# A two-layer sequence model on one core: the second stream yields after each whole-array product, scans weigh less in the mix, and the experts' gate rows come by repeating transfers

## The chip, the cores and the metric

The kernel runs on one core of a Trainium2 chip. Five engines work side by side: TensorE for matrix products (PE, its weight loads are shown as PEld), VectorE (DVE), ScalarE (ACT), GpSimd (POOL) and SyncE (SP), which here only issues transfers. The metric is the device time of one execution in microseconds (us); lower is better. All data are 32-bit floats, except where a product is made in the one-pass format that the code calls F32R.

## The reference

The input is one sequence of 2048 tokens of width 128. Two layers follow, each an attention-like part and a feed-forward part on a residual:

- Layer 0, first part: layernorm, a Mamba-2 style state space block (8 heads of 32, state 16) with a causal convolution of four taps, a gate, a skip path, and an output projection.
- Layer 0, second part: layernorm, causal attention with 16 heads of 8, then layernorm and a mixture of 8 experts of width 512. Every expert is computed for every token. A token's two largest gate logits are put through a softmax and the other six gates are zero, so an expert's output is multiplied by a gate that differs from token to token: `y = sum over e of gate[token, e] * (gelu(x W1[e] + b1[e]) W2[e] + b2[e])`.
- Layer 1, first part: layernorm and a Mamba-1 style scan: 256 channels with 16 states each, `h[t] = exp(-(n+1) delta[t]) * h[t-1] + delta[t] B_n[t] u[t]`, summed over the 16 states, times a gate, and projected.
- Layer 1, second part: layernorm and a feed-forward part of width 512: silu-gated first products, two 512x512 layers with gelu, and a projection to 128.

## The kernel before

**Chunks and stages.** The 2048 tokens are cut into four chunks of 512, numbered 0 to 3. On the chip an activation is held as 128 channels by 512 tokens, so one "whole-array product" is a 128x128 weight against 128x512 activations into one PSUM bank. The stages are Python generators: `ssd(c)` for layer 0's state space block, `attentions()` for all of the attention, `experts(c)`, `scan(c)` and `feed(c)`. At each `yield w` a generator hands over control and says with `w` roughly how much work it has recorded since its last yield. What is recorded then goes through a scheduler that may still move instructions of independent stages past each other, and each engine runs its own list in order.

**Attention is the thread through the middle.** It walks over (chunk, group of four heads). `shift` computes scores once (L302) and takes row maxima on DVE (L312). `weighted` computes scores again, transposed (L352), adds the shift by a product (L358), masks the diagonal (L360), takes `exp` on ACT (L362), and multiplies the result with the values (L339). Each `weighted` step handles two heads by 512 queries by 128 keys. There are 320 such steps over the whole kernel, and only one PSUM buffer, `ps_e`, for their scores, so a step's scores can't be written before the `exp` of the step before has been read out.

**The second stream.** While attention runs, the other stages are mixed in by `with_attention(stages, rate)`: for each `w` that a stage yields, the attention is advanced by `w * rate`. First `ssd(1..3)` are mixed in, then `second_layers()`: `experts(0)`, then `scan(0)` beside `experts(1)`, then `scan(1)` beside `feed(0)`, then `experts(2)`, then `feed(1)`. Two stages are put side by side by `abreast`, which always advances the one that has done the smaller share of its total. When attention is over, the tail runs: `scan(2)` beside `experts(3)`, `scan(3)` beside `feed(2)`, then `feed(3)` alone. Chunk 3's experts need the whole attention; `scan(3)` needs `experts(3)` and the last states of `scan(2)`; `feed(3)` needs `scan(3)`.

**One expert** (in `experts`) loads its weights (256 KB each, L780 and L781), makes four first products (L789) with a `gelu` each (L790), yields 3.7, makes four second products into one bank (L794), multiplies by the gates (L796), adds to the sum on POOL (L798), and yields 3.5. The gates lie with tokens on partitions; the multiplication needs one expert's gates as a row repeated over all 128 partitions. Before, that is made on TensorE: the gates are transposed twice over (L762), split into a high and a low part (L772, L773) so that the one-pass format loses nothing, kept as 16 rows (`rows_in`, L774), and for each expert a one-pass product with a column of ones and zeros (`spread_row`, L719) fills a PSUM bank that DVE copies out (`gb`, L785). `scan` gets its rows `bb` in another way: it writes them to DRAM once (`scratch_b`, L840) and reads each back with a transfer whose source row is repeated for all partitions (L861).

**Tables.** `gelu` and `silu` on the one side and `exp` on the other need different ACT tables, and each change is an ACT_TABLE_LOAD. `in_turn` keeps the recorded order between `gelu` and `exp`, so that they don't alternate at will; how often the recorded order alternates is up to the yields.

**Queues.** SP issues all weight loads, `scratch_b` and `bb` in order; a transfer that waits for its buffer holds up those behind it. POOL issues the transfers that accumulate the scan's sums in SBUF (L876).

Of the kernel before, what the change touches and what calls it, by code (L numbers as in the profile page):

```python
# [12 lines left out]
F32 = mybir.dt.float32  # L13
# [6 lines left out]
P = 128  # L20
# [52 lines left out]
def two_layers(ctx: ExitStack, tc: tile.TileContext, a: dict, out: bass.AP):  # L73
# [375 lines left out]
    attending_all = attentions()  # L449

    SSD, MOE, SCAN, FEED = 43.0, 62.0, 46.0, 40.0
    RATE = (4 * 11.0 + sum(48.0 * (c + 1) for c in range(NC))) / (2.5 * SSD + 2 * (MOE + SCAN + FEED) + 0.6 * MOE)


    with ExitStack() as first:
# [233 lines left out]

    w_eg = load(wp, "w_eg", [P, NE])  # L690
    w_in1 = load(wp, "w_in1", [P, 4 * P])
    w_bd = load(wp, "w_bd", [P, 2, 3 * DS], "(k p) o -> p k o", p=P)
    w_u = load(wp, "w_u", [P, 2, DI], "(k p) o -> p k o", p=P)
    w_dt1 = load(wp, "w_dt1", [3 * DS, DI])
    w_out1 = load(wp, "w_out1", [P, 2, D], "(k p) o -> p k o", p=P)

    halo1 = wp.tile([P, 2, 3], F32, name="halo1")
# [1 line left out]
    hlast = wp.tile([P, 2, DS], F32, name="hlast")  # L699
    nc.gpsimd.memset(hlast, 0.0)  # L700


    zeros = side.line("zeros")
    nc.gpsimd.memset(zeros, 0.0)
    two_rows, minus_low, rows_in = {}, {}, {}
    scratch_b = [tc.dram_tile([DS, C], F32, name=f"scratch_b{i}") for i in range(2)]
    for n in (NE,):
        two_rows[n] = wp.tile([P, n], F32R, name=f"two_rows{n}")
        nc.vector.tensor_tensor(two_rows[n], ident[:, 0:n], ident[:, n : 2 * n], ALU.add)
        minus_low[n] = wp.tile([2 * n, 2 * n], F32R, name=f"minus_low{n}")  # L710
        nc.vector.tensor_scalar(minus_low[n], ident[0 : 2 * n, 0 : 2 * n], 0.0, None, ALU.mult)
        nc.vector.tensor_scalar(minus_low[n][:, n:], ident[0 : 2 * n, n : 2 * n], -1.0, None, ALU.mult)
        rows_in[n] = [wp.tile([P, C], F32R, name=f"rows_in{n}_{i}") for i in range(1)]
        for t in rows_in[n]:
            nc.vector.tensor_copy(t, zeros)

    def spread_row(pg, n, rows_of, i):

        nc.tensor.matmul(pg, two_rows[n][:, i : i + 1].to_broadcast([P, P]), rows_of, start=True, stop=True)  # L719


    def experts(c, z):
        yield from after_stage(("attention", c))
        x = xc[c]
        nx = z.blocks("xn")
        layernorm(nx, xa[c])
        pt = transposed(nx, z.bank)
        nT = z.line("nT")
        nc.vector.tensor_scalar(nT, pt, col("ln2_w"), col("ln2_b"), ALU.mult, ALU.add)
        yield 1.0  # L730

# [24 lines left out]
        nc.vector.reciprocal(top, top)  # L756
        ge2 = sp.tile([P, NB, 2, NE], F32, tag="ge2", name="ge2")
        for i in range(2):
            nc.vector.tensor_tensor(ge2[:, :, i], ge, top.unsqueeze(2).to_broadcast([P, NB, NE]), ALU.mult)
        pgt = z.bank([2 * NE, C])  # L760
        for b in range(NB):
            nc.tensor.matmul(  # L762
                pgt[:, b * P : (b + 1) * P],
                ge2[:, b].rearrange("p i e -> p (i e)"),
                ident,
                start=b == 0,
                stop=True,
                skip_group_check=b > 0,
            )
        gT = rows_in[NE][0]  # L770
        ghi = z.line("ghi", (2 * NE, C), F32R)
        nc.vector.tensor_copy(ghi, pgt)  # L772
        nc.tensor.matmul(pgt, minus_low[NE], ghi, start=False, stop=True, skip_group_check=True)  # L773
        nc.vector.tensor_copy(gT[0 : 2 * NE], pgt)  # L774
        yield 1.5

        acc = z.line("acc")
        for e in range(NE):
            we = z.wide()
            nc.sync.dma_start(we[:, 0], a["fc1"][e])  # L780
            nc.sync.dma_start(we[:, 1].rearrange("p (k d) -> p k d", k=NF), a["fc2"][e].rearrange("(k p) d -> p k d", p=P))  # L781
            pg = z.bank([P, C])
            spread_row(pg, NE, gT, e)
            gb = z.line("gb")
            nc.vector.tensor_copy(gb, pg)  # L785
            hs = [z.four("h") for _ in range(2)]
            for f in range(NF):
                ph = z.bank([P, C])
                nc.tensor.matmul(ph, we[:, 0, f * P : (f + 1) * P], nT, start=True, stop=True)  # L789
                in_turn("gelu", nc.scalar.activation(hs[f // 2][:, f % 2, :], ph, AF.Gelu, bias=col("fc1_b", e * NF + f)))  # L790
            yield 3.7
            py = z.sum([P, C])
            for f in range(NF):
                nc.tensor.matmul(py, we[:, 1, f * P : (f + 1) * P], hs[f // 2][:, f % 2, :], start=f == 0, stop=f == NF - 1)  # L794
            dst = acc if e == 0 else z.line("ye")
            nc.vector.scalar_tensor_tensor(dst, py, col("fc2_b", e), gb, ALU.add, ALU.mult)  # L796
            if e:
                nc.gpsimd.tensor_tensor(acc, acc, dst, ALU.add)  # L798
            yield 3.5
        pt = z.bank([P, NB, D])  # L800
        for b in range(NB):
            nc.tensor.transpose(pt[:, b, :], acc[:, b * P : (b + 1) * P], ident)
        nc.vector.tensor_tensor(x, x, pt, ALU.add)
        yield 1.0


    def scan(c, z):
# [22 lines left out]
            nc.scalar.activation(xs[:, j, :], xs[:, j, :], AF.Silu, bias=col("conv_b", j))  # L830
        yield 4.5

        pb = z.bank([3 * DS, C])
        for k in range(2):
            nc.tensor.matmul(pb, w_bd[:, k, :], xs[:, k, :], start=k == 0, stop=k == 1)
        bd = z.line("bd", (3 * DS, C))
        nc.vector.tensor_scalar(bd, pb, col("bd_b", 0, 3 * DS), None, ALU.add)

        rows_b = scratch_b[c % 2]
        nc.sync.dma_start(rows_b, bd[0:DS])  # L840
# [55 lines left out]
    def feed(c, z):  # L896
# [12 lines left out]
        for f in range(NF):  # L909
# [4 lines left out]
            s = z.line("s")  # L914
            in_turn("gelu", nc.scalar.activation(s, p1, AF.Silu, scale=col("w1_s", f)))
            nc.vector.scalar_tensor_tensor(h[f // 2][:, f % 2, :], p2, col("w2_s", f), s, ALU.mult, ALU.mult)
        yield 7.0
        for name, scale in (("h1", "h1_s"), ("h2", "h2_s")):
            w = []
            for i in range(2):  # L920
# [3 lines left out]
            for f in range(NF):  # L924
                ph = z.bank([P, C])
                for k in range(NF):
                    nc.tensor.matmul(  # L927
                        ph, w[k // 2][:, k % 2, f * P : (f + 1) * P], h[k // 2][:, k % 2, :], start=k == 0, stop=k == NF - 1
                    )
                in_turn("gelu", nc.scalar.activation(g[f // 2][:, f % 2, :], ph, AF.Gelu, scale=col(scale, f)))  # L930
                if f % 2:
                    yield 7.0
            h = g
        po = z.sum([P, NB, D])
        for b in range(NB):
# [9 lines left out]

    def abreast(*threads):

        live = [[g, n, 0.0] for g, n in threads]
        while live:
            for t in sorted(live, key=lambda t: t[2] / t[1]):  # L950
                try:
                    w = next(t[0])
                except StopIteration:
                    live.remove(t)
                    break
                if w is not None:
                    t[2] += w
                    yield w
                    break
            else:  # L960
                yield None

    def second_layers():
        yield from experts(0, side)
        yield from abreast((scan(0, scans), SCAN), (experts(1, side), MOE))
        yield from abreast((scan(1, scans), SCAN), (feed(0, side), FEED))
        yield from experts(2, side)
        yield from feed(1, side)

# [12 lines left out]
def _layout(L0_attn_u, **w):  # L982
# [12 lines left out]
    W_in = w["L0_attn_W_in"]  # L995
    Wqkv, bqkv = w["L0_ffn_Wqkv"], w["L0_ffn_bqkv"]
    x_proj, x_b = w["L1_attn_x_proj_w"], w["L1_attn_x_proj_b"]
    order = np.r_[DS : 2 * DS, DS : 2 * DS, 0:DS]
    bd_b = np.zeros((P, 1), f)
    bd_b[: 3 * DS, 0] = x_b[order]  # L1000
    w_dt1 = np.zeros((3 * DS, DI), f)
    w_dt1[2 * DS :] = w["L1_attn_dt_proj_w"]
    col = {
        "ln_gamma": cols(w["L0_attn_ln_gamma"]),
        "ln_beta": cols(w["L0_attn_ln_beta"]),
# [73 lines left out]
```

## Time and profile before

| | before |
|---|---|
| median of 3 runs | 1753.18 us (1751.92 to 1757.4) |
| the profiled execution's own time | 1741.55 us |
| its span from first to last instruction | 1739.8 us |
| granted TensorE clock, mean | 0.837 |
| busy share of the span: PE, PEld, DVE, ACT, POOL | 84%, 36%, 56%, 42%, 16% |
| attention's last add to the residual (L396) starts at | 1420.0 us |
| transfers | 83.24 MB, mean 48 GB/s |

The profiled execution is 0.67% quicker than the median, so a sum made against the profile is carried to the median by that factor. The shares are means over stages with different limits; the end of the attention at 1420 us cuts the execution in two parts that have to be read apart. A busy PE is not a PE at full speed[...].

### The profile page before, as it was taken

The page shows a single profiled execution, that of the slowest core. Times are in us where ns is not written, and L with a number is a line of the kernel's source. Part 1 is how long each engine was busy: PE and PEld are TensorE (multiplying, and loading weights), DVE is VectorE, ACT ScalarE, POOL GpSimd, SP SyncE. Part 2 cuts the span into 40 slices and gives each one's busy share as a digit, 9 for nine tenths or more (in the row PEclk, how much of TensorE's full clock was granted, in tenths as well). Part 3 has the DMA queues.
Part 4 walks back from the last instruction along what each step waited for, and adds up shares of the span by engine and source line. Part 5 has one row for each costly group of instructions (what it writes and reads, how often), then busy time and mean ns, then how long its engine had stood idle before and what let it go on. Part 6 is the DMA issues. An engine that isn't in the chain of part 4 may idle for free. (4 is left out here: it accounts for less than half of the span.)

```text
span 1739.8 us, 16427 instructions
## 1 busy us (share of the span) xinstructions
PE 1466.9 (84%) x6306; PEld 633.5 (36%) x6306; DVE 975.0 (56%) x1556; ACT 726.2 (42%) x847; POOL 284.0 (16%) x316
## 2 busy tenths in 40 slices
PE   6898999998999888888978887789999888658528
PEld 3554545444333333232333322433333233223214
DVE  4566646557344565667466686674442036774950
ACT  2222322322445444555354454355563536534522
POOL 3322210211000100112111021110000001440220
PEclk9898997887899978889677898669996899868859
DMA  2000000001000000324220045320011022860841
GB/s 85 1 1 1 1 1 1 1 1 55 24 25 25 25 13 21 83 49 103 55 49 14 30 99 107 68 42 25 24 37 31 24 67 78 178 125 31 188 96 30
DMA packets 62494, 83.24 MB, mean 48 GB/s; under 512 B 4576, under 2 KB 28816, under 8 KB 62416
## 3 DMA queue, kind: packets, MB, share of 16 engines
q0 software_dynamic: 16320, 31.46, 10.4%
q1 hardware_dynamic: 45664, 49.68, 9.7%
q8 instruction: 49, 0.80, 0.2%
q10 hardware_dynamic: 432, 1.06, 0.2%
q14 instruction: 29, 0.24, 0.0%
HBM read 49.55 MB, written 1.18 MB: 29 GB/s over the span
## 5 line engine op out<-in xcount | busy, mean ns | idle before, releaser
L362 ACT ACTIVATE probs<-ps_e 128x1024 f32<-128x1024 f32 (+3 forms) x320 | 286.6, 896 | 505.8 <-PE ps_e L358 304.0
L312 DVE TENSOR_REDUCE top<-ps_m 128x2 f32<-128x1024 f32 (+3 forms) x320 | 339.7, 1062 | 280.8 <-PE ps_m L302 164.1
L302 PE MATMUL ps_m<-kR,qR 32*128 32x512 f32 (+3 forms) x640 | 190.1, 523 | 68.0 <-DVE top L312 55.2
L352 PE MATMUL ps_e<-qR,kR 32*128 32x512 f32 (+3 forms) x640 | 175.5, 519 | 27.5 <-ACT probs L362 26.8
L339 PE MATMUL ps_o<-probs,vv 128*9 128x512 f32 (+3 forms) x1152 | 169.7, 599 | 1.0 <-ACT probs L362 0.9
L302 PEld LDWEIGHTS ps_m<-kR,qR 32*128 32x128 f32 x640 | 78.6, 208 | 242.9 <-DVE top L312 132.1
L867 DVE TENSOR_TENSOR_SCAN db<-da,hlast,db 128x512 f32<-128x512 f32 x128 | 163.0, 1310 | 6.5 <-ACT da L863 4.7
L358 PE MATMUL ps_e<-sh,onesR 32*128 32x512 f32 (+3 forms) x640 | 148.9, 431 | 0.0
L352 PEld LDWEIGHTS ps_e<-qR,kR 32*128 32x128 f32 x640 | 69.7, 204 | 182.0 <-ACT probs L362 106.3
L789 PE MATMUL ps_a<-nT,wide 128*128 128x512 f32 x192 | 113.8, 699 | 6.0 <-ACT h L790 3.7
L794 PE MATMUL ps_c<-h,wide 128*128 128x512 f32 x192 | 103.5, 643 | 0.0
L798 POOL TENSOR_TENSOR acc<-acc,ye 128x512 f32<-128x512 f32 x28 | 43.6, 1558 | 331.5 <-DVE ye L796 331.5
L871 POOL COPY hlast<-db 128x2 f32<-128x2 f32 x48 | 29.4, 612 | 378.9 <-DVE db L867 378.9
L863 ACT ACTIVATE da<-dl 128x1024 f32<-128x1024 f32 x64 | 66.4, 1054 | 51.5 <-DMA db<-db 28.3
L865 DVE TENSOR_TENSOR db<-du,bb 128x1024 f32<-128x1024 f32 x64 | 77.9, 1227 | 16.3 <-issue 11.0
L790 ACT ACTIVATE h<-ps_a,cols 128x512 f32<-128x512 f32 x96 | 63.8, 686 | 52.2 <-PE ps_a L789 51.9
L358 PEld LDWEIGHTS ps_e<-sh,onesR 32*128 32x128 f32 x640 | 77.2, 219 | 3.2 <-issue 1.8
L927 PE MATMUL ps_a<-g,wide 128*128 128x512 f32 x96 | 54.0, 690 | 19.5 <-ACT g L930 19.5
L789 PEld LDWEIGHTS ps_a<-nT,wide 128*128 128x128 f32 x192 | 37.1, 215 | 46.3 <-issue 19.5
L362 ACT ACT_TABLE_LOAD x41 | 52.6, 1283 | 1.3 <-PE ps_e L358 0.6
L927 PE MATMUL ps_a<-h,wide 128*128 128x512 f32 x96 | 51.1, 665 | 0.8 <-ACT g L930 0.8
L375 DVE COPY os<-ps_o 128x512 f32<-128x512 f32 x16 | 10.9, 684 | 70.8 <-PE ps_o L339 70.7
(375 smaller groups left out, 2129.3 us busy)
## 6 DMA issues: line engine op xcount, KB each, us to landing
wide<-in_fc SPq DMA_DIRECT2D x64, 256.0 KB, 3.2
bb<-scratch_b SPq DMA_DIRECT2D x64, 256.0 KB, 3.5
db<-db POOLq DMA_DIRECT2D x32, 512.0 KB, 5.7
u<-db POOLq DMA_DIRECT2D x28, 512.0 KB, 6.0
wide<-in_h SPq DMA_DIRECT2D x16, 512.0 KB, 3.7
wide<-in_w SPq DMA_DIRECT2D x8, 256.0 KB, 3.1
x<-in_x SPq DMA_DIRECT2D x4, 256.0 KB, 5.1
w<-in_w SPq DMA_DIRECT2D x4, 256.0 KB, 4.0
```

Of the source, the lines that this page charges most:

```text
L302: nc.tensor.matmul(pss[:, j, 0:n], qR[hr, w - P : w], kR[hr, g, kc * C : kc * C + n], start=True, stop=not diag,)
L312: nc.vector.tensor_reduce(top[:, i : i + 2, kc], pss[:, :, 0:n], AX.X, ALU.max)
L339: pv = nc.tensor.matmul(o, v, prs[i // 2][:, i % 2, q0:], start=kb == 0, stop=kb == nk - 1)
L352: nc.tensor.matmul(pss[:, j, q0:], kR[hr, g, kb * P : (kb + 1) * P], qR[hr, q0:], start=True, stop=False)
L358: nc.tensor.matmul(pss[:, j, q0:], onesR[hr], sh[hr, q0:], start=False, stop=not diag)
L362: last = nc.scalar.activation(pr[:, :, q0:], pss[:, :, q0:], AF.Exp, scale=float(1.0 / np.sqrt(np.float32(HD))))
L789: nc.tensor.matmul(ph, we[:, 0, f * P : (f + 1) * P], nT, start=True, stop=True)
L794: nc.tensor.matmul(py, we[:, 1, f * P : (f + 1) * P], hs[f // 2][:, f % 2, :], start=f == 0, stop=f == NF - 1)
L863: in_turn("exp", nc.scalar.activation(da, dl, AF.Exp, scale=-float(n + 1)))
L865: nc.vector.tensor_tensor(db, du, bb.unsqueeze(1).to_broadcast(two), ALU.mult)
L867: nc.vector.tensor_tensor_scan(db[:, j, :], da[:, j, :], db[:, j, :], hlast[:, j, n : n + 1], ALU.mult, ALU.add)
L927: nc.tensor.matmul(ph, w[k // 2][:, k % 2, f * P : (f + 1) * P], h[k // 2][:, k % 2, :], start=k == 0, stop=k == NF - 1)
```

## The change

It has three parts. First, `experts` and `feed` yield after each whole-array product in a group that accumulates (0.9 each, 0.8 after the last), where they yielded 3.5 or 7.0 after a group; the totals stay the same. Second, `abreast` takes a share for each thread, and what it passes on to the mix with the attention is `w` times the share: 0.3 for scans, 1.0 for the others. The rate is worked out anew from these: it was 524 / 440.7 = 1.19 and becomes 524 / 401.1 = 1.31. The tail's `together` has no shares. Third, the gates are transposed once (8 rows), written to DRAM (`scratch_g`, 16 KB), and each expert reads its row with a transfer that repeats it over the 128 partitions, issued by SP after the expert's two weight loads. The products and copies of `spread_row` go, and so do the high and low parts, and the doubled rows that `w_bd` and `w_dt1` still had (48 rows become 32).

```diff
-    RATE = (...) / (2.5 * SSD + 2 * (MOE + SCAN + FEED) + 0.6 * MOE)
+    RATE = (...) / (2.5 * SSD + 3 * MOE + 0.6 * SCAN + 2.0 * FEED)
...
-    def spread_row(pg, n, rows_of, i):
-        nc.tensor.matmul(pg, two_rows[n][:, i : i + 1].to_broadcast([P, P]), rows_of, start=True, stop=True)
+    scratch_g = [tc.dram_tile([NE, C], F32, name=f"scratch_g{i}") for i in range(2)]
...  experts: the gates
-        ge2 = sp.tile([P, NB, 2, NE], F32, tag="ge2", name="ge2")
-        for i in range(2):
-            nc.vector.tensor_tensor(ge2[:, :, i], ge, top.unsqueeze(2).to_broadcast([P, NB, NE]), ALU.mult)
-        pgt = z.bank([2 * NE, C])
-        for b in range(NB):
-            nc.tensor.matmul(pgt[:, b * P : (b + 1) * P], ge2[:, b]..., ident, ...)
-        gT = rows_in[NE][0]
-        ghi = z.line("ghi", (2 * NE, C), F32R)
-        nc.vector.tensor_copy(ghi, pgt)
-        nc.tensor.matmul(pgt, minus_low[NE], ghi, start=False, stop=True, skip_group_check=True)
-        nc.vector.tensor_copy(gT[0 : 2 * NE], pgt)
+        nc.vector.tensor_tensor(ge, ge, top.unsqueeze(2).to_broadcast([P, NB, NE]), ALU.mult)
+        pgt = z.bank([NE, C])
+        for b in range(NB):
+            nc.tensor.transpose(pgt[:, b * P : (b + 1) * P], ge[:, b], ident)
+        gT = z.line("gT", (NE, C))
+        nc.vector.tensor_copy(gT, pgt)
+        gates = scratch_g[c % 2]
+        nc.sync.dma_start(gates, gT)
...  experts: one expert
-            pg = z.bank([P, C])
-            spread_row(pg, NE, gT, e)
             gb = z.line("gb")
-            nc.vector.tensor_copy(gb, pg)
+            nc.sync.dma_start(gb, gates[e].partition_broadcast(P))
...
                 nc.tensor.matmul(py, we[:, 1, f * P : (f + 1) * P], ...)
+                if f < NF - 1:
+                    yield 0.9
...
-            yield 3.5
+            yield 0.8
...  feed: the first products
-        yield 7.0
+            if f % 2:
+                yield 3.5
...  feed: h1 and h2
                     nc.tensor.matmul(ph, w[k // 2][:, k % 2, f * P : (f + 1) * P], ...)
+                    if k < NF - 1:
+                        yield 0.9
                 in_turn("gelu", nc.scalar.activation(g[f // 2][:, f % 2, :], ph, AF.Gelu, scale=col(scale, f)))
-                if f % 2:
-                    yield 7.0
+                yield 0.8
...  abreast
-                    t[2] += w
-                    yield w
+                    t[3] += w
+                    yield w * t[2]
...
-        yield from abreast((scan(0, scans), SCAN), (experts(1, side), MOE))
-        yield from abreast((scan(1, scans), SCAN), (feed(0, side), FEED))
+        yield from abreast((scan(0, scans), SCAN, 0.3), (experts(1, side), MOE, 1.0))
+        yield from abreast((scan(1, scans), SCAN, 0.3), (feed(0, side), FEED, 1.0))
```

More of the change, by code (lines that the diff above doesn't have):

```diff
@@ L451, in two_layers @@
     SSD, MOE, SCAN, FEED = 43.0, 62.0, 46.0, 40.0
-    RATE = (4 * 11.0 + sum(48.0 * (c + 1) for c in range(NC))) / (2.5 * SSD + 2 * (MOE + SCAN + FEED) + 0.6 * MOE)
+    RATE = (4 * 11.0 + sum(48.0 * (c + 1) for c in range(NC))) / (2.5 * SSD + 3 * MOE + 0.6 * SCAN + 2.0 * FEED)
     with ExitStack() as first:
@@ L691, in two_layers @@
     w_in1 = load(wp, "w_in1", [P, 4 * P])
-    w_bd = load(wp, "w_bd", [P, 2, 3 * DS], "(k p) o -> p k o", p=P)
+    w_bd = load(wp, "w_bd", [P, 2, 2 * DS], "(k p) o -> p k o", p=P)
     w_u = load(wp, "w_u", [P, 2, DI], "(k p) o -> p k o", p=P)
-    w_dt1 = load(wp, "w_dt1", [3 * DS, DI])
+    w_dt1 = load(wp, "w_dt1", [2 * DS, DI])
     w_out1 = load(wp, "w_out1", [P, 2, D], "(k p) o -> p k o", p=P)
@@ L700, in two_layers @@
     nc.gpsimd.memset(hlast, 0.0)
-    zeros = side.line("zeros")
-    nc.gpsimd.memset(zeros, 0.0)
-    two_rows, minus_low, rows_in = {}, {}, {}
+    scratch_g = [tc.dram_tile([NE, C], F32, name=f"scratch_g{i}") for i in range(2)]
     scratch_b = [tc.dram_tile([DS, C], F32, name=f"scratch_b{i}") for i in range(2)]
[L707 to L715, printed above, removed]
-    def spread_row(pg, n, rows_of, i):
-        nc.tensor.matmul(pg, two_rows[n][:, i : i + 1].to_broadcast([P, P]), rows_of, start=True, stop=True)
     def experts(c, z):
@@ L756, in experts @@
         nc.vector.reciprocal(top, top)
-        ge2 = sp.tile([P, NB, 2, NE], F32, tag="ge2", name="ge2")
-        for i in range(2):
-            nc.vector.tensor_tensor(ge2[:, :, i], ge, top.unsqueeze(2).to_broadcast([P, NB, NE]), ALU.mult)
-        pgt = z.bank([2 * NE, C])
+        nc.vector.tensor_tensor(ge, ge, top.unsqueeze(2).to_broadcast([P, NB, NE]), ALU.mult)
+        pgt = z.bank([NE, C])
         for b in range(NB):
[L762 to L769, printed above, removed]
-        gT = rows_in[NE][0]
-        ghi = z.line("ghi", (2 * NE, C), F32R)
-        nc.vector.tensor_copy(ghi, pgt)
-        nc.tensor.matmul(pgt, minus_low[NE], ghi, start=False, stop=True, skip_group_check=True)
-        nc.vector.tensor_copy(gT[0 : 2 * NE], pgt)
+            nc.tensor.transpose(pgt[:, b * P : (b + 1) * P], ge[:, b], ident)
[3 more added lines that the diff above has]
+        nc.sync.dma_start(gates, gT)
         yield 1.5
@@ L831, in scan @@
         yield 4.5
-        pb = z.bank([3 * DS, C])
+        pb = z.bank([2 * DS, C])
         for k in range(2):
             nc.tensor.matmul(pb, w_bd[:, k, :], xs[:, k, :], start=k == 0, stop=k == 1)
-        bd = z.line("bd", (3 * DS, C))
-        nc.vector.tensor_scalar(bd, pb, col("bd_b", 0, 3 * DS), None, ALU.add)
+        bd = z.line("bd", (2 * DS, C))
+        nc.vector.tensor_scalar(bd, pb, col("bd_b", 0, 2 * DS), None, ALU.add)
         rows_b = scratch_b[c % 2]
@@ L946, in abreast @@
     def abreast(*threads):
-        live = [[g, n, 0.0] for g, n in threads]
+        live = [[g, n, share, 0.0] for g, n, share in threads]
         while live:
-            for t in sorted(live, key=lambda t: t[2] / t[1]):
+            for t in sorted(live, key=lambda t: t[3] / t[1]):
                 try:
@@ L997, in _layout @@
     x_proj, x_b = w["L1_attn_x_proj_w"], w["L1_attn_x_proj_b"]
-    order = np.r_[DS : 2 * DS, DS : 2 * DS, 0:DS]
+    order = np.r_[DS : 2 * DS, 0:DS]
     bd_b = np.zeros((P, 1), f)
-    bd_b[: 3 * DS, 0] = x_b[order]
-    w_dt1 = np.zeros((3 * DS, DI), f)
-    w_dt1[2 * DS :] = w["L1_attn_dt_proj_w"]
+    bd_b[: 2 * DS, 0] = x_b[order]
+    w_dt1 = np.zeros((2 * DS, DI), f)
+    w_dt1[DS:] = w["L1_attn_dt_proj_w"]
     col = {
```

## The prediction

> **What bounds the kernel now.** I read the cores' spans first, then the busy table by stage, then waits, groups, and the timeline where the attention ends.
>
> ```profile
> core 0: 1739.8 us, clock 0.837
> ```
> ```profile
> core 0: us, PE busy (x) PEld busy (x) DVE busy (x) ACT busy (x) POOL busy (x), PEclk, DMA share, GB/s
> 455.00:700.00 245.00, 224.44 (x967) 85.88 (x966) 129.46 (x212) 113.83 (x131) 17.96 (x19) 0.88 0.09 26
> 700.00:900.00 200.00, 175.23 (x697) 64.94 (x693) 121.92 (x137) 95.73 (x109) 30.09 (x32) 0.77 0.30 63
> 900.00:1170.00 270.00, 221.84 (x1059) 89.66 (x1057) 192.23 (x252) 126.81 (x133) 45.10 (x49) 0.78 0.29 63
> 1170.00:1300.00 130.00, 124.80 (x584) 45.53 (x582) 57.95 (x67) 74.20 (x83) 7.65 (x6) 0.96 0.10 29
> 1300.00:1420.00 120.00, 108.38 (x445) 38.99 (x445) 18.00 (x40) 55.37 (x61) 3.79 (x4) 0.82 0.09 25
> 1420.00:1570.00 150.00, 102.82 (x246) 44.57 (x244) 105.28 (x139) 74.90 (x81) 53.69 (x46) 0.81 0.55 127
> 1570.00:1690.00 120.00, 60.78 (x154) 28.23 (x154) 81.24 (x94) 51.01 (x52) 25.01 (x21) 0.76 0.53 114
> ```
>
> The rows are the experts of chunk 0, the two stages with scans (to 1170), experts of chunk 2, `feed(1)`, and two tail stages. From 455 to 1420 PE is busy 854.7 of 965 us (89%): PE leads, at a clock between 0.77 and 0.96. In the tail it is 69% and then 51% busy, and DVE leads. So PE work is dear before 1420 and cheap after.
>
> ```profile
> ACT probs L362 <- PE ps_e L358: 304.0, 148, 11.6
> PEld ps_e L352 <- ACT probs L362: 106.3, 111, 4.3
> ```
> ```profile
> 1362.12 1.02 ACT L362 ACTIVATE probs<-ps_e 128x1024 f32<-128x1024 f32 x1 [0.88 <-PE ps_e L358]
> 1363.16 1.28 ACT L930 ACT_TABLE_LOAD   x1
> ...
> 1364.46 1.27 ACT L930 ACTIVATE g<-ps_a,cols 128x512 f32<-128x512 f32 x2
> ...
> 1365.74 1.28 ACT L362 ACT_TABLE_LOAD   x1
> ```
>
> Scores and `exp` take turns on one buffer, so whatever holds ACT holds PE's next scores: here two gelus cost ACT 3.9 us, 2.57 of it tables.
>
> ```profile
> 1418.07 1.16 PE L394 MATMUL ps_e<-w_o,aT 128*128 128x128 f32 x8
> ...
> 1440.17 0.52 PE L719 MATMUL ps_m<-rows_in,two_rows 128*128 128x512 f32 x1
> 1440.53 1.02 PE L789 MATMUL ps_e<-nT,wide 128*128 128x512 f32 x2
> ```
> ```profile
> 1452.01 0.75 DVE L796 SCALAR_TENSOR_TENSOR acc<-ps_o,cols,gb 128x512 f32<-128x512 f32 x1 [2.88 <-PE ps_o L794]
> 1452.67 0.68 DVE L785 COPY gb<-ps_e 128x512 f32<-128x512 f32 x1
> ```
>
> The attention ends at 1420, but the last experts' first product waits until 1440.5 behind `feed(1)`'s last products, `scan(2)`'s start, the gates and the row product.
>
> **The change part by part.** The instruction order of the two built programs shows what moves; durations are from the profile.
>
> *Rows by transfers.* Before the tail this takes from PE 24 row products (14.0 us, 584 ns each), 3 low-part products (0.604 each) and half of the gates' transposes (12 of 24 records, 0.421 us): up to 20 us of busy time, less where records overlap. From DVE it takes 24 copies (16.3 us). PE is 89% busy at 0.84 clock, but some of the removed work lies where PE would have waited for `exp`: I take -10, from 0 to -20. It adds 32 reads of 256 KB and 4 writes on SP. The nearest rows are `bb` (256 KB, 3.5 us to landing, 6.5 at most; 0.33 us of issue) and `scratch_b` (1.6 us). A gate row is needed only after an expert's eighth product, about 7 us after it starts; the eight products cover it. Without that cover, an expert waits some 3 us. Behind a waiting gate row on SP stand the next weights and `bb`; they have two buffers and more in hand. POOL's queue is not passed.
>
> *Yields after each product.* The order says that this does little: of 255 attention steps that hold second-stream work, or could, 103 have none before and 101 after. The scheduler already spread most products singly. I take -2 (0 to -15).
>
> *Table loads.* The finer yields cut the gelus of `feed` into single ones. ACT's order holds 130 table loads before and 160 after: 91 and 119 until the last attention `exp`, 39 and 41 behind it. So 28 more, 35.9 us of ACT at 1.283 us, in 14 more gelu blocks. ACT is busy 465.9 of those 965 us, so it has room, but each block delays one `exp` by 2.57 us while PE holds perhaps 1.5 us of other work: about 0.9 us per block, +13 (0 to +36). The Trainium skill speaks against the change more strongly: "ScalarE: Activation LUTs", What ACT_TABLE_LOAD costs, adds a drain of about 1.38 us to each load, 2.66 us per switch, which would be 74 us of ACT for the 28, and about +32 in my sum (the delay per block grows by 2.7 us, half of it on PE). The row above shows no drain (`exp` ends 1363.14, load 1363.16 to 1364.44, gelu 1364.46), so I keep 1.283.
>
> *Weights of the mix.* Scans draw 0.3 of their former attention, everything else 10% more (1.31 to 1.19). The scan stages get shorter and denser, the experts' lighter. Total attention stays. The order shows the effect at the seam: `feed(1)` ends before the attention does, and `scan(2)`'s start (10 products up to softplus) slips in ahead of the attention's end. Moved into the attention: 10 products, and 6 products and nine 128-column ones of `feed(1)`; at 0.86 us each for two full-clock records, and 2 us, about 16 us. PE's idle time of 12 us in 1300 to 1420 takes part: +10 (+4 to +19).
>
> So the attention ends later by -10 - 2 + 13 + 10 = +11 us.
>
> *The tail.* Now PE's list behind the attention has the experts' transposes, two gate-logit groups, then at once the first expert's products: they start perhaps 8 us after the attention instead of 20.5. The first multiply still needs gates: 8 us to logits, 8.3 us of gate arithmetic (1428 to 1436.3 now), 1.5 of transposes, 0.7 of copy, then 1.6 and 3.5 us of transfers with 0.7 of issue: +24, where it is now +32 (1452). That is -8. `scan(2)`'s first `da` is now 42 us after the attention's end (1461.8); with its start done and two experts ahead of it in ACT's order it comes at about 26: -16. Seven gate copies leave DVE between the multiplies (7 x 0.68 = -4.8); DVE leads there. The stage ends with the later of experts and scan, and both gain: 8 + 5 = 13 for the one, up to 16 + 5 = 21 for the other. The scan was last (its residual add at 1569.5, the experts' at 1550.8): I take -19 (-4 to -32). `scan(3)` beside `feed(2)` and `feed(3)`: nearly the same orders, 0.
>
> Sum against the profiled execution: 1741.55 + 11 - 19 = 1733.5. The median is 1.0067 times the profile, so 1745.
>
> *Clock.* "TensorE: Matmul & The Clock Gate", What's actually happening, lets the clock fall only after an idle window of about 3.4 us. By that rule a kernel this dense would run at 1.0 and smoother filling gains nothing. The stage rows disagree: 0.77 at 88% busy, 0.96 at 96%. So more even filling might gain; if the stages from 700 to 1170 went from 0.78 to 0.82, their 397 busy us would lose about 20. I take 0 and keep -25.
>
> **The rivals.** A, likeliest: the sum, faster, 1728 to 1748. 36%.
>
> B: the seam merely moves. Every microsecond taken from the tail comes back in the attention (+19 for the moved work, its upper end, with the rest in balance): 1753. 17%. For it: total work changes by a few us only.
>
> C, slower: table loads. If every load in the attention stands on the path, +36 in place of +13 gives 1756.5 in the profile, 1768 in the median. It decides from 1.5 us per block (14 x 1.5 = 21, where the total is zero). Its places are `feed(0)`, `feed(1)` and `experts(1)`, where gelus now come singly. For it: the 304 us that `exp` and scores wait for each other; against: ACT is 48% busy. 25%.
>
> D, slower: rows come late in the tail, where DMA is already 0.55 busy and the rows stand on SP behind weight loads that wait for PE. At the price of 3 us in each of 8 experts, +24: 1757.5, so 1769. 12%.
>
> E: the clock gains 25: 1708, so 1720. 10%.
>
> **How the numbers follow.** Faster: A and E, 0.46. Slower: C and D, 0.37. Same, B: 0.17, with "same" as 0.3% (5 us), about what a measurement of this kernel can tell from no change. The range takes in E's and C's and D's points and the ends of the tail's term: 1714 to 1780; A's own stands above.
>
> **What would show it.** Right: the last residual add of the attention (L396) at 1425 to 1440; the last experts' first product within 10 us of it; scan and experts of that stage done some 19 us sooner after it; more than 155 table loads at 1.28 us; no wait for `gb` but at the first expert. The sum is wrong if the attention ends before 1415 (E) or after 1450 (C: look at scores waiting for `exp`), or if the multiply waits for `gb` in every tail expert (D).

## The result and the profile after

The changed kernel takes 1741.64 us (median of 20 runs, 1731.06 to 1748.65); the kernel before, run in turn with it, 1756.2 us (20 runs, 1740.97 to 1768.0). The ratio is 0.9919, with a 95% interval from 0.9902 to 0.9935: 14 us faster, where 8 were predicted. In this ratio and in those below, runs more than 1.5% above the quickest of the same kernel are left out. The two kernels' runs overlap, and the profiles caught them at opposite ends: the profiled execution of before (1741.55 us) is quicker than all but one of its 20 runs, that of after (1748.65 us) is the slowest of its own. So the two profiles stand 7 us the wrong way round, and a difference between them has to be judged by how well it comes back in a second profile. The spans:

```profile
core 0: 1746.9 us, clock 0.839
```

Busy time by stage, after (the columns are those of the same table of before; the boundaries follow after's own stages from 1300 on, with the attention's end at 1443):

```profile
core 0: us, PE busy (x) PEld busy (x) DVE busy (x) ACT busy (x) POOL busy (x), PEclk, DMA share, GB/s
455.00:700.00 245.00, 219.53 (x983) 84.88 (x981) 123.12 (x215) 115.39 (x133) 16.50 (x17) 0.90 0.14 40
700.00:900.00 200.00, 171.28 (x685) 64.11 (x685) 129.58 (x147) 108.44 (x121) 34.42 (x40) 0.82 0.38 88
900.00:1170.00 270.00, 227.48 (x997) 90.31 (x997) 179.23 (x233) 136.83 (x144) 39.15 (x45) 0.81 0.28 63
1170.00:1300.00 130.00, 120.32 (x573) 44.69 (x568) 60.06 (x80) 73.24 (x80) 10.20 (x9) 0.96 0.13 41
1300.00:1443.00 143.00, 118.91 (x572) 44.48 (x570) 36.02 (x48) 80.09 (x82) 1.27 (x1) 0.84 0.08 25
1443.00:1575.00 132.00, 82.82 (x172) 35.95 (x172) 85.56 (x106) 62.64 (x69) 46.83 (x45) 0.76 0.63 146
1575.00:1697.00 122.00, 67.20 (x152) 30.53 (x152) 81.56 (x93) 60.44 (x59) 25.09 (x21) 0.78 0.52 112
```

The first tail stage is 132 us long, where it had 150. ACT has more to do in the two stages with scans (together 245 us, was 223) and in the last one of the attention (80 us of 143, was 55 of 120). The clock of the two stages with scans is 0.82 and 0.81, was 0.77 and 0.78; it is lower in the first tail stage. PE still leads until the attention's end.

Scores and `exp`, in the table of waits (total us, times, longest), and the same alternation in ACT's timeline inside `feed(1)`:

```profile
ACT probs L362 <- PE ps_e L358: 293.2, 139, 17.3
...
PEld ps_e L352 <- ACT probs L362: 111.8, 128, 3.7
```
```profile
1375.03 1.02 ACT L362 ACTIVATE probs<-ps_e 128x1024 f32<-128x1024 f32 x1 [0.89 <-PE ps_e L358]
1376.07 1.28 ACT L907 ACT_TABLE_LOAD   x1
1377.37 0.69 ACT L907 ACTIVATE g<-ps_a,cols 128x512 f32<-128x512 f32 x1
1378.07 1.28 ACT L362 ACT_TABLE_LOAD   x1
1379.36 1.02 ACT L362 ACTIVATE probs<-ps_e 128x1024 f32<-128x1024 f32 x1
```

In the place that the prediction shows, two gelus shared one such pair of loads; here a single one has it. There are 160 loads, 119 of them before the attention's end, as the instruction order said. The total that PE's scores wait for `exp` has grown by only 5.5 us (106.3 to 111.8), although the number of these waits grew from 111 to 128.

The seam, PE's timeline and the first expert's multiply on DVE:

```profile
1440.31 2.08 PE L394 MATMUL ps_e<-w_o,aT 128*128 128x128 f32 x8 [0.78 <-DVE aT L391]
1446.33 1.16 PE L165 MATMUL ps_e<-ident,xn 128*128 128x128 f32 x4 [3.94 <-DVE xn L157]
1448.39 1.88 PE L718 MATMUL ps_m<-w_eg,nT 128*128 128x8 f32 x8 [0.91 <-DVE nT L713]
1450.55 2.08 PE L761 MATMUL ps_m<-nT,wide 128*128 128x512 f32 x2 [0.28 <-DVE lg L720]
```
```profile
1458.71 0.68 DVE L746 COPY gT<-ps_e 8x512 f32<-8x512 f32 x1 [1.59 <-PE ps_e L744]
1465.09 0.75 DVE L770 SCALAR_TENSOR_TENSOR acc<-ps_o,cols,gb 128x512 f32<-128x512 f32 x1 [5.70 <-PE ps_o L766]
```

The attention's last add to the residual starts at 1443.2. The first expert's product starts 7.4 us after it, ahead of the gates and no longer behind them. The gates are ready at 1459.4; the row is written, read back and there before the expert's own second products are done, so the multiply is released by PE (`ps_o`) and not by a transfer. The table of the attention's end and of what comes after it, in us from the attention's end (ends of the adds and multiplies, starts of the others):

| | before | after |
|---|---|---|
| attention's last residual add starts at | 1420.0 | 1443.2 |
| first product of the last experts | +20.5 | +7.4 |
| first gate multiply | +32.7 | +22.6 |
| `scan(2)`'s first `da` | +41.7 | +26.7 |
| residual add of the experts | +131.4 | +116.4 |
| residual add of `scan(2)` | +150.1 | +132.2 |
| residual add of `scan(3)` | +266.5 | +251.0 |
| end | +319.8 | +303.8 |

One profile each can't say which rows of this table are the kernel's and which the execution's. So both kernels were profiled a second time.

### The profile page after: what moved, and what is told of

Its sections match the earlier page's. It is cut to its first block, busy times and chain, and to the rows that moved or that the text cites. A ratio compares the mean times of both kernels' runs of the same rounds, so it can differ in the third digit from the quotient of the medians.

```text
span 1746.9 us, 16374 instructions
## 1 busy us (share of the span) xinstructions
PE 1464.4 (84%) x6254; PEld 637.5 (36%) x6254; DVE 956.2 (55%) x1512; ACT 765.1 (44%) x877; POOL 274.4 (16%) x315
## 5 line engine op out<-in xcount | busy, mean ns | idle before, releaser
L302 PE MATMUL ps_m<-kR,qR 32*128 32x512 f32 (+3 forms) x640 | 181.3, 505 | 54.5 <-DVE top L312 45.6
L352 PE MATMUL ps_e<-qR,kR 32*128 32x512 f32 (+3 forms) x640 | 167.1, 508 | 31.6 <-ACT probs L362 29.7
L339 PE MATMUL ps_o<-probs,vv 128*9 128x512 f32 (+3 forms) x1152 | 162.3, 574 | 2.8 <-ACT probs L362 2.8
L358 PE MATMUL ps_e<-sh,onesR 32*128 32x512 f32 (+3 forms) x640 | 141.5, 417 | 0.8 <-DVE sh L324 0.8
L352 PEld LDWEIGHTS ps_e<-qR,kR 32*128 32x128 f32 x640 | 66.0, 200 | 187.2 <-ACT probs L362 111.8
L902 PE MATMUL ps_a<-g,wide 128*128 128x512 f32 x96 | 66.6, 827 | 19.3 <-ACT g L907 14.4
L845 POOL COPY hlast<-db 128x2 f32<-128x2 f32 x48 | 20.5, 426 | 381.9 <-DVE db L841 376.3
L358 PEld LDWEIGHTS ps_e<-sh,onesR 32*128 32x128 f32 x640 | 72.1, 211 | 4.6 <-issue 3.4
```

What stands on the lines that cost most here:

```text
L302: nc.tensor.matmul(pss[:, j, 0:n], qR[hr, w - P : w], kR[hr, g, kc * C : kc * C + n], start=True, stop=not diag,)
L339: pv = nc.tensor.matmul(o, v, prs[i // 2][:, i % 2, q0:], start=kb == 0, stop=kb == nk - 1)
L352: nc.tensor.matmul(pss[:, j, q0:], kR[hr, g, kb * P : (kb + 1) * P], qR[hr, q0:], start=True, stop=False)
L358: nc.tensor.matmul(pss[:, j, q0:], onesR[hr], sh[hr, q0:], start=False, stop=not diag)
L902: nc.tensor.matmul(ph, w[k // 2][:, k % 2, f * P : (f + 1) * P], h[k // 2][:, k % 2, :], start=k == 0, stop=k == NF - 1)
```

## The experiments

Ratios are against the kernel before in the same comparison. "Attention" below is a difference: the ratio's share of 1753 us, less the change of the tail in the profile. Times after the attention's end come from the profile of each kernel. The clock is the median of the timed runs (the kernel before, run beside the experiments: 0.828 to 0.830).

| kernel | ratio [95%] | median us | loads in attention, behind | tail us (319.8 before) | attention us | clock |
|---|---|---|---|---|---|---|
| after | 0.9919 [0.9902, 0.9935] | 1741.64 | 119, 41 | 303.8 | +2 | 0.839 |
| mix_only | 1.0074 [1.0047, 1.0101] | 1763.78 | 104, 32 | 316.0 | +17 | 0.836 |
| rows_only | 0.9912 [0.9878, 0.9945] | 1738.18 | 91, 39 | 314.0 | -10 | 0.831 |
| yields_only | 1.0031 [1.0008, 1.0054] | 1758.61 | 103, 46 | 327.5 | -2 | 0.830 |
| rows_mix | 0.9861 [0.9826, 0.9895] | 1726.0 | 102, 34 | 303.6 | -8 | 0.847 |
| rows_tail_mix | 0.9951 [0.9933, 0.9970] | 1745.98 | 104, 34 | 301.3 | +10 | 0.838 |
| rows_att_mix | 0.9987 [0.9963, 1.0011] | 1748.48 | 102, 32 | 316.0 | +1 | 0.836 |
| tables_more | 0.9924 [0.9883, 0.9965] | 1754.7 | 126, 34 | 303.2 | | 0.833 |
| rows_mix_expyields | 0.9884 [0.9852, 0.9917] | 1732.13 | 102, 34 | 305.4 | -6 | 0.837 |
| rows_mix_coarse | 1.0007 [0.9983, 1.0031] | 1749.58 | 92, 30 | 310.3 | +11 | 0.830 |
| row_products_unread | 0.9838 [0.9806, 0.9870] | 1728.12 | 102, 32 | 299.7 | -8 | 0.842 |

How far to trust the column "attention": `rows_tail_mix` has `mix_only`'s order in the attention, and still the column says +10 for the one and +17 for the other. So it is good to some 7 us.

### The two kernels once more: before_again and after_again

Nothing is edited.

> The kernel before, unchanged, for a second profile. The first profile's execution (1741.55 us) is shorter than the median of 20 later ones (1756.2). If only the attention's part varies: a tail of 320 us again, within 3, and the attention's end between 1425 and 1440. If the tail varies too, the tails of the other profiles can't be compared one by one.

> The changed kernel, unchanged, for a second profile; the first one's execution (1748.65 us) is the longest of its 20. If only the attention's part varies: a tail of 304 us again, within 3, and the attention's end between 1425 and 1440, so that the attention takes as long as before and the change's gain is the tail's.

The cores of before's second profile, and of after's:

```profile
core 0: 1756.6 us, clock 0.826
```
```profile
core 0: 1739.1 us, clock 0.842
```

The attention ends at 1436.5 (was 1420.0) in the kernel before, and at 1436.1 (was 1443.2) in the changed one: the same orders, 16.5 and 7 us apart, and equal in the second pair. The tails are 320.1 (319.8) and 302.9 (303.8) us. The first multiply is at +32.7 both times before and at +22.6 both times after. So the -16 us of the tail belong to the change, and the +23 us of the attention's end in the first pair of profiles do not. What differs between two executions is how long TensorE's products take. These are the rows of the kernel before, up to its attention's end, in its first profile and in its second:

```profile
0.00:1420.00 1420.00, 1260.43 (x5794) 540.93 (x5795) 783.63 (x1318) 590.80 (x701) 204.03 (x248) 0.84 0.14 35
```
```profile
0.00:1436.50 1436.50, 1279.42 (x5795) 553.27 (x5796) 783.50 (x1318) 591.17 (x701) 204.16 (x249) 0.83 0.14 34
```

PE is busy for 19.0 us more with the same products, and idle for 159.6 and 157.1 us; DVE and ACT have the same busy time. The clock is lower in the longer one. Over 40 timed runs of before, a line through time and mean clock falls by 12 us for each hundredth, over another 51 by 9 us.

### mix_only: the shares and the rate alone

An edit of the kernel before; `scan(1)` beside `feed(0)` has the same shares, and `abreast` multiplies by them as in the change.

```diff
-    RATE = ... / (2.5 * SSD + 2 * (MOE + SCAN + FEED) + 0.6 * MOE)
+    RATE = ... / (2.5 * SSD + 3 * MOE + 0.6 * SCAN + 2.0 * FEED)
-        yield from abreast((scan(0, scans), SCAN), (experts(1, side), MOE))
+        yield from abreast((scan(0, scans), SCAN, 0.3), (experts(1, side), MOE, 1.0))
```

> The kernel before with the weights of the mix alone (scans at 0.3, the rate at 1.31); gate rows still by products, coarse yields. In the instruction order this alone moves scan(2)'s start and the end of feed(1) ahead of the attention's end (table loads 104 before and 32 behind the last attention exp). Seam theory: the attention ends some 10 us later, the tail is 12 to 16 us shorter, 1 to 8 us faster in all (ratio 0.995 to 0.999). Rows theory, that the gate rows carry the whole gain: 1.000. Clock theory, that more even filling carries it: the gain of 0.8% stays here only if the attention ends no later.

A miss: slower by 0.74%, not faster. The tail is only 3.8 us shorter, and the attention term is +17. Most of the tail's gain is missing. One part is missing at the seam, where the first product of the last experts is still late, now for another reason. PE's timeline there:

```profile
1438.64 1.88 PE L734 MATMUL ps_m<-w_eg,nT 128*128 128x8 f32 x8 [0.90 <-DVE nT L729]
1444.12 1.87 PE L762 MATMUL ps_e<-ident,ge 128*16 128x128 f32 x8 [3.60 <-DVE ge L759]
1446.76 0.60 PE L773 MATMUL ps_e<-ghi,minus_low 16*16 16x512 f32 x1 [0.77 <-DVE ghi L772]
1448.13 0.80 PE L719 MATMUL ps_m<-rows_in,two_rows 128*128 128x512 f32 x1 [0.77 <-DVE rows_in L774]
1448.72 1.91 PE L789 MATMUL ps_e<-nT,wide 128*128 128x512 f32 x2
```

`scan(2)`'s start is out of the way, but in PE's list the row product (L719) stands ahead of the first expert's products, and it needs the gates: gate arithmetic, transposes, low parts, two copies. PE waits 3.60, 0.77 and 0.77 us and reaches the first product at +15.3. In the changed kernel only the multiply needs the gates. The other part goes while the experts run: the first multiply comes 7 us sooner after the attention's end than in the kernel before, and `scan(2)`'s first `da` 10 us, but the last multiply less than 4 us (+123.9, was +127.5).

### rows_only: the gate rows by transfers alone

The kernel before with the third part of the change and nothing else, the gates' single transposing and `scratch_g` included.

```diff
-            spread_row(pg, NE, gT, e)
-            nc.vector.tensor_copy(gb, pg)
+            nc.sync.dma_start(gb, gates[e].partition_broadcast(P))
```

> The kernel before with the gate rows by transfers alone. Seam theory: PE loses its 32 row products and DVE its copies, 10 us less in the attention and some 5 to 8 in the last experts: 10 to 18 us faster (0.990 to 0.994); less if PE waits for exp where the products stood. Rows theory: the whole gain, 0.992. Late-rows theory: the multiplies of the last experts wait for gb, 1.000 or above.

0.9912: this part alone gives as much as the whole change. About 6 us of it are in the tail, 10 in the attention. At its seam, the other half of the obstacle remains (lines left out are marked):

```profile
1422.24 0.83 PE L909 MATMUL ps_c<-w,g 128*128 128x128 f32 x6
...
1423.18 3.17 PE L909 MATMUL ps_c<-w,g 128*128 128x128 f32 x26
...
1427.73 1.98 PE L792 MATMUL ps_a<-nT,w_in 128*128 128x512 f32 x4 [0.62 <-DVE nT L786]
1429.55 0.95 PE L718 MATMUL ps_m<-w_eg,nT 128*128 128x8 f32 x8
1434.76 2.07 PE L761 MATMUL ps_m<-nT,wide 128*128 128x512 f32 x2 [4.26 <-DVE lg L720]
```

`feed(1)`'s last products (L909) and `scan(2)`'s first (L792) still lie between the attention and the experts, and the first expert starts at +12.4 (from 1422.3). The longest wait in it, 4.26 us, is for a copy on DVE (`lg`, the gate logits), which stands there behind `scan(2)`'s convolution.

### rows_mix: both of these, without the finer yields

An edit of the changed kernel; `feed` gets back the yields of before likewise.

```diff
-                if f < NF - 1:
-                    yield 0.9
...
-            yield 0.8
+            yield 3.5
```

> The changed kernel without the yields after each product: rows and mix alone. 136 table loads against 160 of the changed kernel (102 and 34 against 119 and 41). Table theory: the 17 loads saved in the attention and 7 in the tail make it faster than the changed kernel by 8 to 15 us, so 0.983 to 0.988 against before. Theory that the yields carry the gain: slower than the changed kernel, 0.996. If yields do nothing: 0.992.

0.9861, 1726.0 us: it beats both kernels, and its interval lies clear of the changed kernel's. The tail is as short as the changed kernel's (303.6), the first product at +7.4, the first multiply at +23.0, the first `da` at +27.0. So the whole of the tail's gain needs rows and mix together: the rows alone bring 6 us, the mix alone 4, both 16. The first product stands behind two things, and there the two parts simply add: the rows bring it forward by 8 us, the mix by 5, both by 13. What exceeds the sum comes afterwards, while eight experts run beside `scan(2)`. From the first gate multiply to the last it takes 95 us in the kernel before, 92 with the rows, 98 with the mix and 88 with both (one profile of each). The fine yields give none of it.

### rows_tail_mix and rows_att_mix: the rows' gain cut in two

Against `rows_mix`: `rows_tail_mix` uses the transfer only for the last chunk's experts, as the diff shows, and `rows_att_mix` only for the other three chunks' (`c < NC - 1`). The gates are prepared to match, and both kernels keep the doubled rows of `w_bd` and `w_dt1`.

```diff
+            if c == NC - 1:
                 nc.sync.dma_start(gb, gates[e].partition_broadcast(P))
+            else:
+                spread_row(pg, NE, gT, e)
+                nc.vector.tensor_copy(gb, pg)
```

> Mix as in the changed kernel, coarse yields; gate rows by transfers for the last experts (chunk 3) alone, by products in the attention. Between mix_only (1.0074) and rows_mix (0.9861) lie 37 us, of which the profiles show 12 in the tail (tail 316.0 and 303.6). If the tail's part is what the profiles show: 12 us faster than mix_only, 1.000. If rows matter only on the path behind the attention: 0.986.

> The other half: mix and coarse yields, gate rows by transfers for the experts of chunks 0 to 2, inside the attention, by products for chunk 3. Theory that 24 row products and copies stand in PE's and DVE's way beside the attention: 25 us faster than mix_only, 0.993. Theory that the attention hides them: 1.007, as mix_only.

From `mix_only` (1.0074) the tail's half goes to 0.9951, 22 us, and the attention's half to 0.9987, 15 us. Together that is the 37 us to `rows_mix` (0.9861). Neither ratio is one of those expected of it; each half of the rows has a part of the gain. Of the 22 us the profiles show 15 in the tail, and the other 7 are within the error of the column. The first product is at +7.4 in the first and at +15.3 in the second, as in the kernels that they take after.

### row_products_unread: TensorE's part of the rows, alone

An edit of `rows_mix`.

```diff
+            pg = z.bank([P, C])
+            nc.tensor.matmul(pg, two_rows[:, e : e + 1].to_broadcast([P, P]), rows_in, start=True, stop=True)
             gb = z.line("gb")
             nc.sync.dma_start(gb, gates[e].partition_broadcast(P))
```

> rows_mix with the 32 row products put back on PE (zeros as rows, into the same PSUM bank), but not the copies on DVE: the gates still come by transfers and nobody reads the products. If PE's time is the price of the rows: 14 us of products in the attention cost 8 to 14 us, 0.991 to 0.994. If the price is the copy, which waits on DVE behind the scan and the row maxima and holds the bank: 0.986 to 0.988.

The groups of its page have the 24 row products of the attention back, 551 ns each where they took 584:

```profile
L763 PE MATMUL ps_a<-rows_in,two_rows 128*128 128x512 f32 x24 | 13.2, 551 | 0.0
```

And the time is 0.9838 [0.9806, 0.9870], against 0.9861 [0.9826, 0.9895] without them: they cost nothing that can be measured (by the two intervals, 4 us at the most). What the rows by transfers save is therefore not the row products' time on TensorE. What is left are the copies on DVE, the bank that is held until the copy, the products' wait for the gates, and the low parts and transposes, which were not put back. In the tail the bank can be seen. The groups of the kernel before, in the stage from 1420 to 1570 (the last column: idle time before them, and what ended it):

```profile
L789 PE MATMUL ps_m<-nT,wide 128*128 128x512 f32 x32 | 23.2, 815 | 11.3 <-DVE gb L785 8.9 <-ACT h L790 2.4
L789 PE MATMUL ps_e<-nT,wide 128*128 128x512 f32 x32 | 22.0, 778 | 15.5 <-DVE gb L785 10.5 <-ACT h L790 5.1
```

The experts' first products waited 19.4 us for `gb`'s copy to leave a bank, since the copy stood in DVE's list among the scan's long instructions. The same groups of `mix_only`, in the 150 us after its attention's end:

```profile
L789 PE MATMUL ps_e<-nT,wide 128*128 128x512 f32 x32 | 24.1, 847 | 15.6 <-DVE gb L785 13.3 <-ACT h L790 2.3
L789 PE MATMUL ps_m<-nT,wide 128*128 128x512 f32 x32 | 22.1, 778 | 13.8 <-DVE gb L785 9.9 <-ACT h L790 3.9
```

Here the wait is 23.2 us: with the mix alone the products start sooner and meet the copy all the same. With the transfers these waits are gone; the same products then wait 32.1 us for gelus (`h`) in `rows_mix`, so the length of the wait is not its price. In the attention PE's products wait for the copy only 2.1 us, so there it is not the bank. Whether it is the copies' 16 us on DVE, among the row maxima that the scores need, or the gate chain was not separated.

### yields_only: the finer yields alone

An edit of the kernel before, in `experts`; `feed` has the finer yields of the change too.

```diff
                 nc.tensor.matmul(py, we[:, 1, f * P : (f + 1) * P], ...)
+                if f < NF - 1:
+                    yield 0.9
...
-            yield 3.5
+            yield 0.8
```

> The kernel before with the yields after each product alone. The instruction order has 149 table loads against 130 (103 and 46). Table theory: 12 more loads in the attention at some 0.5 us of PE's time each, and 7 more in the tail: 6 to 12 us slower (1.003 to 1.007). Theory that finer pieces fill PE more evenly: faster, 0.995. If both are small: 1.000.

1.0031, some 5 us slower, as the theory of the tables expected, but not where it expected it: the column "attention" has -2, and the tail is 8 us longer. It has 12 more loads in the attention than the kernel before and 7 more behind it, and its first product comes at +24.3. On top of `rows_mix` the same edit makes the changed kernel: from 0.9861 to 0.9919, 10 us slower, with 17 more loads in the attention and 7 behind it and an unchanged tail (303.6 and 303.8), so that there the cost lies in the attention.

### rows_mix_expyields: the finer yields in the experts only

An edit of `rows_mix`; `feed` is unchanged.

```diff
+                if f < NF - 1:
+                    yield 0.9
-            yield 3.5
+            yield 0.8
```

> The changed kernel with the finer yields in the experts alone; feed yields as before. It has the 136 table loads of rows_mix. Table theory: the experts' yields are free, 0.986 as rows_mix, and the 10 us that the yields cost come from feed. If finer pieces fill PE better where they bring no loads: 0.982. If interleaving itself costs: 0.989 or above.

0.9884, with no more loads than `rows_mix` (136), and inside its interval. Of the yields' 10 us the medians put 4 on those in the experts and 6 on those in `feed`, the ones that make more table loads; either figure has an error of some 6 us. That points to the loads, but does not show them, since an order changes too.

### tables_more: the loads by themselves

An edit of `rows_mix`, in `weighted`.

```diff
+                if c and i == 0 and kb % 8 == 5:
+                    in_turn("gelu", nc.scalar.activation(tiny, ones[:, 0:1], AF.Gelu))
```

> rows_mix with a gelu of one column after every eighth key block's exp of chunks 1 to 3: its result is used by nothing. The instruction order has 126 table loads in the attention against 102, in 12 more blocks; each block holds ACT 2.57 us for loads and some 0.2 us for the gelu. Table theory, at the 0.9 us per block of the prediction: 11 us slower than rows_mix, 0.992. If every load is on the path: 31 us slower, 1.004. If ACT has room for them: 0.986, and the price of the yields is not the tables.

Its runs spread from 1725.07 to 1761.48 us, and the ratio of 0.9924 rests on the 5 quickest of its 14; the median of all 14 is 1754.7, 1.0007 of the kernel before's. So 12 more blocks of two loads cost 11 us by the one and 26 us by the other: between 0.9 and 2.1 us for each block. The prediction's 0.9 is the lower end. The direction is shown, the size isn't. Its tail is 303.2 us, as that of `rows_mix`.

### rows_mix_coarse: fewer loads

An edit of `rows_mix`, in `feed`'s inner layers; the new yield follows the loop over the four groups.

```diff
-                if f % 2:
-                    yield 7.0
+            yield 14.0
```

> rows_mix with feed's two inner layers yielding once for four gelus instead of twice: 92 and 30 table loads against 102 and 34. Table theory: 5 blocks fewer in the attention at 0.9 us, so 4 us faster than rows_mix, 0.984. If the bursts of 16 products that come with it starve the attention's exp: 0.990 or above.

The table theory alone misses here: 10 loads fewer in the attention and 4 fewer behind it, and the kernel is 26 us slower (1.0007 against 0.9861). The other expectation came true, of 0.990 or above with 16 products recorded between two turns of the attention. Its tail is 7 us longer; the rest is in the attention, with a clock of 0.830 where `rows_mix` has 0.847. Whether the longer waits of the attention lower the clock or the lower clock makes the waits isn't settled. Of the three grains of `feed`'s yields that were tried, one yield for each two groups is clearly better than the coarser one, and by the medians 6 us better than the finer one, which is within the error.

## Why the prediction was right, point by point

The sum was 8 us faster, and the result is 14. The mechanism of the tail held step by step, within 1 to 3 us; of the attention's four terms two had another cause or size than the prediction gave. The nearness of the sum is in part luck: the tail brought 3 us less than forecast and the attention cost 9 us less, and these two errors partly offset each other. The prediction gave "faster" 46%, and its range of 1714 to 1780 us would have held a slower kernel too.

**The tail, -19: right.** It measures -16.0, and -17.2 in the second pair of profiles. The steps: first product at about 8 us (7.4), start of the first multiply at +24 (+21.9), first `da` at +26 (+26.7), experts -13 (-15.0), scan last and up to -21 (-17.9). `scan(3)` and what follows was costed at 0 and is +1.9. What the prediction did not see is that this needs two parts of the change at once. It read the seam from the final order and did not ask which part does what: the rows let the products go ahead of the gates and take the copies away, the mix takes `scan(2)`'s start out of the way.

**Rows by transfers in the attention, -10: right size, wrong reason.** `rows_only` has -10 there and `rows_att_mix` 15 us less than `mix_only`. The step argued from 20 us of TensorE's busy time at 89% load; `row_products_unread` puts 13 us of that back at no cost. A stage's busy share is no price: PE leads there, and still these products cost nothing. That they lay where PE would have waited anyway, as the prediction allowed for some of them, fits this but is not shown.

**Finer yields and table loads, -2 and +13: right sign and size on top of the other two parts.** Together +11, measured +10 (`rows_mix` to after). On the kernel before, the same yields cost nothing in the attention (-2) and 8 us in the tail, where the prediction had no term. The -2 in itself has no support. The price of a block, 0.9 us, is the lower end of what `tables_more` shows. By its own terms (2.57 us less 1.5) it should have been 1.07, and the +13 a +15. "ScalarE: Activation LUTs", What ACT_TABLE_LOAD costs, in the Trainium skill would add a drain of 1.38 us to each load; in the timeline above `exp` ends at 1376.05, the load starts at 1376.07 and the gelu follows it by 0.02 us, so no drain is seen in the kernel after either; 144 of its 160 loads start within 0.1 us of the end of ACT's work before them.

**Work moved into the attention by the mix, +10: not confirmed as a constant.** Alone the mix has +17 in the attention; on top of the rows, 1 or 2 (from `rows_only`'s -10 to `rows_mix`'s -8, within the column's error). The argument counted moved products and their time and would give the same in both. Why the mix is dear with the row products and free without them stays open.

**The attention's end: right number, weak test.** "1425 to 1440" was to be read from one profile, and 1443.2 and 1436.1 are two profiles of the same kernel; before, it is 1420.0 and 1436.5. By difference of medians the attention is +2, where +11 was summed: the 9 us are the term of the mix.

**The rivals.** B (the seam merely moves) fell with the tail: it came back in the attention only for `mix_only`. C (all loads on the path) did not decide: the finer yields with their loads cost 10 us here, where C needs 21 to cancel the gain. The 304 us that it quoted for itself speak for nothing of the kind: they are `exp` waiting for scores. The wait the other way round, in which a held-up ACT would show, is the 106.3 us below them. D (late rows) did not occur: no multiply waits for `gb`. E expected the stages with scans at 0.82 and has its row: 0.82 and 0.81. The 20 us that it drew from this can't be checked there, since the same stretch now holds other work (PE busy for 398.8 us, was 397.1). The timed runs of the kernels with the mix and a yield of 7.0 or finer have a mean clock of 0.833 to 0.847, those without the mix 0.828 to 0.831. But the clock does not rank the kernels: `mix_only` has 0.836 and is 13 us slower than before, `rows_only` has 0.831 and is 15 us faster. How much of the 14 us goes through the clock can't be told from these runs, since no run holds the clock fixed.

## What to carry over

When a stage is held up by two things, look for both before one is removed: each alone brought 4 and 6 us here, both 16. And follow the gain to the stage's end: at the first product the two added up, and the rest was won or lost behind it. Price removed work by putting it back unread where that can be done: a busy share of 89% said 10 us for rows whose products measure as nothing. How the rest of their price divides between copies, held banks and gates is open. And fine yields are only worth their table loads up to a point: leave out the part of this change that yields after each product, and the kernel takes 1726 us in place of 1742.

## What had not been expected of the hardware

The same instruction orders on one core end their attention 16.5 us apart in two executions, at a mean clock of 0.837 and 0.826, and the kernel before spreads from 1736 to 1769 us over its runs. The clock is below full even where TensorE is busy most of the time: 0.81 in after's stage from 900 to 1170 with 227.5 of 270 us busy, 0.96 in the next at 120.3 of 130.

The traces also record when the clock changes. In all 14 it is either full or half, and it changes at multiples of 3.41 us. Take the stretches of 3.41 us at full clock between 455 and 1420 us, and the share of each in which PE was busy (rough, since the ends of products are modelled). Of the 238 stretches under 60%, 235 were followed by half clock; of the 594 from 60 to 90%, 102; of the 1945 above 90%, none. At half clock, none of the 426 stretches under 80% was followed by full clock, and 328 of the 755 above were. An example from the kernel after:

```profile
1410.05:1413.46 3.41, 2.57 (x14) 0.59 (x6) 1.40 (x2) 2.75 (x4) 0.00 (x0) 1.00 0.20 59
1413.46:1416.88 3.42, 1.92 (x14) 0.53 (x14) 1.32 (x2) 3.37 (x4) 0.00 (x0) 1.00 0.15 49
1416.88:1420.29 3.41, 1.55 (x6) 0.63 (x6) 3.31 (x5) 1.70 (x3) 0.00 (x0) 0.50 0.00 0
```

PE is busy for 75% of the first stretch and 56% of the second, and the third runs at half clock. The Trainium skill's "TensorE: Matmul & The Clock Gate", What's actually happening, ties a fall to an idle window of about 3.4 us; here 316 of 337 falls follow a stretch without any idle time as long as that (the longest is 1.3 us in the median). So in this kernel it matters for the clock how evenly PE is filled from one such stretch to the next, and not only its busy share over a stage. Why the same orders fill them differently in two executions is not shown.

And the tail, in whose stages PE is busy for 51 to 69% of the time, comes back within 1 us in each pair of profiles, where the attention's end moves by 7 and 16.5 us: a difference of a few us can be read from the profile of the tail, and not from that of the attention.
